# A kernel that plans its own order of issue: the planner's durations taken from a trace, and new ranks of its streams

## The chip, the cores and the metric

The kernel runs on one core of one Trainium2 chip. The metric is the device time of one execution in microseconds (us); the kernel before takes 4853.1 us, the median of three executions (4836.61 to 4856.57). Five engines work side by side on a core, each through its own instructions in the order in which they stand in the program: TensorE (PE, matrix products into the accumulator memory PSUM), VectorE (DVE), ScalarE (ACT), GpSimd (POOL), and SyncE (SP), which here only issues data transfers. An instruction that needs another engine's result waits on a semaphore, and everything behind it in its own engine's queue waits too.

## The reference

The batch is 32 images of 56 x 56 positions with 96 channels, float32. Two layers follow each other. Cut to what matters:

```python
# layer 0: a convolution block with weights mixed per image
pooled = jnp.mean(x, axis=(1, 2))
rw  = sigmoid(pooled @ Wr + br)                       # 4 mixing weights per image
h   = relu(bn(x @ mix(rw, Wpw)))                      # 96 -> 384 channels
h   = relu(bn(depthwise3x3(h, mix(rw, Wdw))))         # 9 taps per channel
x   = x + bn(h @ mix(rw, Wpwl))                       # 384 -> 96
# layer 1: a Fourier block, then a feed-forward net; tokens are the 3136 positions
t = x.reshape(32, 3136, 96)
h = relu(bn(layernorm(t) @ w1))                       # 96 -> 192
X = fft(h, axis=tokens)
xr, xi = relu(X.real*r - X.imag*i + rb), relu(X.imag*r + X.real*i + ib)
t = t + bn(ifft(xr + 1j*xi).real @ w2)                # 192 -> 96
t = t + qlinear(relu(qlinear(layernorm(t), W1)), W2)  # 8-bit products, 96 -> 384 -> 96
```

## The kernel before

Every image passes through a chain of stages. Each stage is written as a Python generator, a *stream*, which yields before each step the engine that the step runs on, the events it needs and the buffers it takes. A small planner, `Plan`, steps through all streams while the program is being built. It keeps a clock per engine, adds an estimated duration for each recorded instruction, and always goes on with the stream whose next step can start earliest; among steps that could start equally early the lower *rank* (called priority) goes first. The order in which the planner takes the steps is the order in which the instructions stand in the program. The planner's clock does not exist on the chip: only its order does.

```python
class Plan:
    HOP = 0.12
    def tick(self, engine, us):
        start = max(self.free[engine], self.now)
        self.now = self.free[engine] = start + us
    def run(self):
        while self.streams:
            for stream in self.streams:
                ...                                   # ready: own step, events, buffers
                key = (max(ready, self.free[stream.engine]), stream.priority, ready)
                if best is None or key < best[0]: best = key, ready, stream
            ...
            self.now = ready
            self._advance(stream)                     # records the step's instructions
```

The estimated durations of the kernel before (n is the number of elements per partition):

```python
if self.engine == DVE:   ...; us = 0.15 + n / 1000.0     # f16 tensor_scalar: n halved
elif self.engine == ACT: us = 0.24 + n / 1250.0
elif self.engine == POOL: us = 0.2 + n * {"tensor_copy": 1.2, "memset": 0.6}.get(name, 2.4) / 1000.0
else:                    us = 0.08                       # SP: issue of a transfer
def arrives(nbytes, *key): plan.done(*key, late=2.5 + nbytes / 150e3)
```

The streams, by the names of the PSUM tiles that their TensorE work fills (these names stand in the profile):

```python
mixing      # DVE: pooled (sum of an image), PE ps_rw, ACT sigmoid, DVE: wk, small, wk2 (mixed weights)
expansion   # PE ps_pw  -> ACT hp            (96 -> 384, two parts p of each image)
tensor      # PE ps_dw  -> ACT h2            (7 of 11 blocks of the depthwise taps: 3 waves of 144 products)
vector      # DVE h2 = hp * weight + h2      (the other taps: 8 per group of blocks, 1792, 1344 or 896 wide)
projection  # PE ps_pwl -> DVE x             (384 -> 96, added to the image)
forward     # PE ps_t_a -> DVE st_a, dm_a -> ACT rstd_a; PE ps_w1 -> DVE ha; PE ps_a -> ACT g -> SP gd
frequencies # SP g2 <- gd; PE ps_b -> ACT z, mir; POOL mir; DVE mir, z; ACT mir; DVE z   (8 halves per image)
spectrum    # PE ps_w2 (needs z) -> ACT zo -> PE ps_c -> DVE zo -> SP yd                 (4 per image)
inverse     # SP yt <- yd; PE ps_d -> DVE x; PE ps_t_f -> ACT, DVE, ACT yt; PE ps_n -> ACT n8
            # PE ps_f1 -> ACT h16 -> DVE h16 -> POOL h8; PE ps_f2 -> ACT y16 -> DVE y16 -> POOL x -> SP out
```

In the profile both `ps_w1` and `ps_w2` stand as `ps_w` (told apart by their inputs), `ps_f1` and `ps_f2` as `ps_f`, and the names lose their image numbers. Buffers are scarce on purpose: four PSUM buffers of two banks, two `mir`, one `zo`, four `h16`, two images' worth of `z`.

```python
plan = Plan(ps=4, mir=2, zo=1, h16=4)
...
Q.dma_start(yds[b][...], zo[:, 0:nk, :])
plan.release("zo", plan.now + 2.0)
...
("loads", 0, loads()), ("mixing", 0, mixing()), ("inverse", 1, inverse(0)),
("inverse", 1, inverse(1)), ("frequency loads", 0, frequency_loads()),
("frequencies", 2, frequencies()), ("forward", 3, forward(0)),
("forward", 3, forward(1)), ("projection", 4, projection()),
("vector", 5, convolved_vector()), ("tensor", 5, convolved_tensor()),
("expansion", 6, expansion()),
```

Of the kernel before, what the change touches and what calls it, by code (L numbers as in the profile page):

```python
# [46 lines left out]
NE = 4  # L47
C = 96
# [81 lines left out]
class Plan:  # L130
# [7 lines left out]
    HOP = 0.12  # L138

    def __init__(self, **buffers):  # L140
        self.free = dict.fromkeys((PE, DVE, ACT, POOL, SP), 0.0)
        self.now = 0.0
        self.events = {}
        self.streams = []

        self.buffers = {tag: [0.0] * n for tag, n in buffers.items()}
        self.busy = dict.fromkeys(self.free, 0.0)

    def tick(self, engine, us):
        start = max(self.free[engine], self.now)  # L150
        self.now = self.free[engine] = start + us
        self.busy[engine] += us
# [14 lines left out]
    def spawn(self, name, priority, gen):  # L167
        stream = Stream(name, priority, gen, self.now + self.HOP)
        self.streams.append(stream)
        self._advance(stream)  # L170

    def _advance(self, stream):
        now = self.now
        try:
            stream.wants(next(stream.gen))
        except StopIteration:
            self.streams.remove(stream)
        stream.ready = self.now + self.HOP
        return now

    def run(self):
        while self.streams:
            best = None
            for stream in self.streams:
                if any(len(self.buffers[tag]) < n for tag, n in stream.takes.items()):
                    continue
                ready = stream.ready
                missing = False
                for key in stream.after:
                    at = self.events.get(key)  # L190
                    if at is None:
                        missing = True
                        break
                    ready = max(ready, at + self.HOP)
                if missing:
                    continue
                for tag, n in stream.takes.items():
                    ready = max(ready, self.buffers[tag][n - 1])
                key = (max(ready, self.free[stream.engine]), stream.priority, ready)
                if best is None or key < best[0]:  # L200
                    best = key, ready, stream
            if best is None:
                raise RuntimeError(
                    "no stream can go on: "
                    + "; ".join(
                        f"{s.name} {[k for k in s.after if k not in self.events]} {s.takes}"
                        for s in self.streams
                    )
                )
            _, ready, stream = best  # L210
            for tag, n in stream.takes.items():
                del self.buffers[tag][:n]
            self.now = ready
            self._advance(stream)


def _size(ap):
    return int(np.prod(ap.shape[1:]))


class Engine:


    def __init__(self, plan, engine, namespace):
        self.plan, self.engine, self.namespace = plan, engine, namespace

    def __getattr__(self, name):
        def issue(out, *args, **kw):
            n = _size(out)
            if self.engine == DVE:  # L230
                if name in ("tensor_reduce", "bn_stats"):
                    n = _size(args[0])
                elif name == "reciprocal":
                    n *= 4
                elif name in ("tensor_scalar", "tensor_copy") and out.dtype == F16:
                    n *= 0.5
                us = 0.15 + n / 1000.0
            elif self.engine == ACT:
                us = 0.24 + n / 1250.0
            elif self.engine == POOL:  # L240
                us = 0.2 + n * {"tensor_copy": 1.2, "memset": 0.6}.get(name, 2.4) / 1000.0
            else:
                us = 0.08
            self.plan.tick(self.engine, us)
            return getattr(self.namespace, name)(out, *args, **kw)  # L245

        return issue


@with_exitstack  # L250
def kernel(
# [227 lines left out]
    def as_halves(ap):  # L479
# [3 lines left out]
    V, A, P, Q = (  # L483
        Engine(plan, DVE, nc.vector), Engine(plan, ACT, nc.scalar),
# [12 lines left out]
    def transpose(to, ap, eye):  # L497
        plan.tick(PE, 0.09)
        nc.tensor.transpose(to, ap, eye)

    def arrives(nbytes, *key):
        plan.done(*key, late=2.5 + nbytes / 150e3)
# [10 lines left out]
    def mixing():  # L513

        for b in range(NB):
# [4 lines left out]
            V.tensor_scalar(pool_b, ones, pooled, 1.0 / N, ALU.mult, ALU.mult)  # L520
# [14 lines left out]
            for e in range(1, NE):  # L535
                V.scalar_tensor_tensor(wk, wpw_s[:, e, :], rw[:C, e : e + 1], wk, ALU.mult, ALU.add)
# [3 lines left out]
            V.tensor_mul(prod, stk_s, by.to_broadcast([128, NMIX, NE + 1]))  # L540
            small = mixp.tile([128, NMIX], F32, tag="small", name=f"small_{b}")
            V.tensor_reduce(small, prod, AX.X, ALU.add)
# [8 lines left out]
            for e in range(1, NE):  # L551
                V.scalar_tensor_tensor(wk2, wpwl_s[:, e], rw[:, e : e + 1], wk2, ALU.mult, ALU.add)
# [30 lines left out]
    def expansion():  # L583

        for b, p, before in parts_of_all():
            xb = xpad[b % 3]
            for c in (2, 0, 1):

                for part, (at, ns) in enumerate(((0, (9, 9)), (18, (8, 8) if p == 0 else (8,)))):
# [10 lines left out]
                    plan.spawn("evac pw", 0, expanded(b, p, c, part, at, ns, ps))  # L600
# [17 lines left out]
    def convolved_tensor():  # L618

        for b, p, before in parts_of_all():  # L620
            for i, wave in enumerate(WAVES[p]):
# [5 lines left out]
                for t in range(9):  # L627
                    w, h = divmod(t, 3)
                    for q, (c, k) in enumerate(wave):
                        for g in range(G):  # L630
# [10 lines left out]
                                share=13.5,  # L641
# [4 lines left out]
                plan.spawn("evac dw", 0, convolved(b, p, i, wave, ps))  # L646
# [15 lines left out]
    def convolved_vector():  # L662

        for b, p, before in parts_of_all():
            for c, k0, nk in ON_VECTOR[p]:
# [6 lines left out]
                for t in range(9):  # L672
# [7 lines left out]
                    else:  # L680
                        V.scalar_tensor_tensor(to3, seen, weight, to3, ALU.mult, ALU.add)
# [39 lines left out]
    def moments(name, xt, s, who, out, kept=None):  # L721
# [21 lines left out]
        V.tensor_sub(d, st[:, :, 1], st[:, :, 4])  # L743
        V.tensor_add(v, st[:, :, 2], st[:, :, 5])
        V.scalar_tensor_tensor(d, d, C / 4.0, d, ALU.mult, ALU.mult)
        V.tensor_add(v, v, d)
# [65 lines left out]
    def frequencies():  # L812

        n = 0
        for b in range(NB):
            for i, (k0, nk) in enumerate(GROUPS):
# [9 lines left out]
                plan.spawn("spectrum", 1, spectrum(n, b, i, k0, nk))  # L826
                n += 1

    def nonlinearity(n, b, k0, nk, h, ps):
# [32 lines left out]
        V.scalar_tensor_tensor(zr, zr, 2.0, mr, ALU.mult, ALU.max)  # L862
        V.scalar_tensor_tensor(zi, zi, 0.0, mi, ALU.max, ALU.subtract)
# [3 lines left out]
    def imaginary_parts(n, h, im, zi, mi, col, used):  # L867
        yield DVE
        V.scalar_tensor_tensor(mi, im, col(nrd), zi, ALU.mult, ALU.add)
        V.scalar_tensor_tensor(zi, im, col("rd"), zi, ALU.mult, ALU.add)  # L870
# [3 lines left out]
    def spectrum(n, b, i, k0, nk):  # L874
# [37 lines left out]
        plan.release("zo", plan.now + 2.0)  # L912
        arrives(4 * PB * GK * C, "yd", b, i)

    def inverse(parity):


        for b in range(NB):
            for s in range(parity, NS, 2):
# [25 lines left out]
                V.tensor_add(nm, st[:, :, 1], st[:, :, 4])  # L945
                V.scalar_tensor_tensor(nm, nm, -0.5, rstd, ALU.mult, ALU.mult)
# [18 lines left out]
                for c in range(NC3):  # L965
# [8 lines left out]
                    plan.spawn("hidden", 0, hidden(parity, b, s, c, ps, h8))  # L974
# [38 lines left out]
    with tc.manual_schedule():  # L1013
        for name, priority, stream in (
            ("loads", 0, loads()), ("mixing", 0, mixing()), ("inverse", 1, inverse(0)),
            ("inverse", 1, inverse(1)), ("frequency loads", 0, frequency_loads()),
            ("frequencies", 2, frequencies()), ("forward", 3, forward(0)),
            ("forward", 3, forward(1)), ("projection", 4, projection()),
            ("vector", 5, convolved_vector()), ("tensor", 5, convolved_tensor()),
# [118 lines left out]
```

## Time and profile before

| | before |
|---|---|
| time, median of 3 | 4853.1 us |
| span of the profiled execution | 4857.6 us, 113896 instructions |
| TensorE (PE) busy | 4384.4 us, 90% |
| VectorE (DVE) busy | 3640.3 us, 75% |
| ScalarE (ACT) busy | 2774.1 us, 57% |
| GpSimd (POOL) busy | 1091.4 us, 22% |
| granted TensorE clock, mean | 0.944 of full speed |
| bytes moved | 339.06 MB, 70 GB/s |

All work of an image is recorded through two helper lines, so the line numbers of the profile say little; the tile names say which stage an instruction belongs to. TensorE's busy time is the union of its matrix products' recorded durations. A product takes longer in the record than it holds up its successor, because products are pipelined, so 90% busy does not say that 10% is all that can be won. Busy time of the other engines is closer to work done.

The waits are inferred: an engine's idle time is put down to whichever semaphore came last. "issue" is time in which an engine waited for nothing the profile shows.

### The profile page before, as it was taken

The numbers are of one execution on the slowest core, as the hardware profiler recorded it, in microseconds if no ns is written. First come the engines' busy times: TensorE is split into PE (matmuls) and PEld (weight loads), VectorE is DVE, ScalarE is ACT, GpSimd is POOL, SyncE is SP. The second block draws the span as 40 slices with busy tenths as digits, with TensorE's granted clock in tenths as the row PEclk, the third lists the DMA queues.
The fourth block names the chain that finished last, engine by engine and source line by source line (L and its number), as shares of the span: only waits on it lengthen the run. The fifth ranks groups of instructions, "written<-read, shape, count | busy, mean of one in ns | idle before, by whom it ended". The sixth has DMA issues, their size and how long they took to land.

```text
span 4857.6 us, 113896 instructions
## 1 busy us (share of the span) xinstructions
PE 4384.4 (90%) x47942; PEld 3137.0 (65%) x47942; DVE 3640.3 (75%) x7474; ACT 2774.1 (57%) x4391; POOL 1091.4 (22%) x1074
## 2 busy tenths in 40 slices
PE   5999989999898999989999899999989999999986
PEld 2666666666666666667666666666666666666664
DVE  5777778777877777867778787777877778687763
ACT  2556556665565655656555566655656556565544
POOL 1021212212122221322212122121222212222122
PEclk9999999999999999999999999999999999999986
DMA  3122223222222222222222232222222222222221
GB/s 83 56 76 70 58 69 84 67 68 70 60 79 73 67 71 72 60 80 75 76 63 65 69 85 66 68 70 60 79 73 68 70 75 62 80 73 73 63 70 43
DMA packets 304472, 339.06 MB, mean 70 GB/s; under 512 B 126836, under 2 KB 243476, under 8 KB 300660
## 3 DMA queue, kind: packets, MB, share of 16 engines
q1 hardware_dynamic: 303960, 331.77, 24.9%
q8 instruction: 377, 6.18, 0.5%
q14 instruction: 135, 1.11, 0.1%
HBM read 163.98 MB, written 158.27 MB: 66 GB/s over the span
## 4 chain that ended last, share of the span: by engine, by line
PE 64%; DVE 16%; ACT 12%; issue 5%; DMA 2%; POOL 0%; SPq 0%; ACTq 0%; POOLq 0%; DVEq 0%
PE ps_dw L495 14%; PE ps_pwl L495 10%; PE ps_pw L495 10%; PE ps_w L495 8%; DVE h L245 6%; PE ps_a L495 5%; PE ps_b L495 5%; PE ps_f L495 4%; DVE z L245 4%; ACT h L245 3%; PE ps_d L495 2%; ACT yt L245 2%; PE ps_c L495 2%; DVE wk L245 2%; DVE mir L245 1%
## 5 line engine op out<-in xcount | busy, mean ns | idle before, releaser
L245 DVE SCALAR_TENSOR_TENSOR h<-hp,small,h 128x1792 f32<-128x1792 f32 (+2 forms) x768 | 1269.7, 1653 | 28.4 <-ACT h L245 14.7
L495 PE MATMUL ps_dw<-hp,diag 32*32 32x448 f32 x27648 | 879.0, 545 | 42.9 <-issue 20.2
L245 POOL CAST h<-h 128x784 fp8e5<-128x784 f16 x384 | 489.7, 1295 | 1356.9 <-DVE h L245 1356.2
L495 PEld LDWEIGHTS ps_dw<-hp,diag 32*32 32x32 f32 x27648 | 536.0, 103 | 336.9 <-issue 121.9
L495 PE MATMUL ps_pw<-x,wk 96*128 96x504 f32 (+1 forms) x1344 | 657.9, 625 | 60.3 <-ACT g L245 35.3
L495 PE MATMUL ps_pwl<-h,wk 128*96 128x448 f32 x1344 | 532.3, 544 | 10.6 <-ACT h L245 10.6
L245 ACT ACTIVATE hp<-ps_pw,small 128x1008 f32<-128x1008 f32 (+2 forms) x384 | 363.3, 960 | 305.1 <-PE ps_pw L495 303.3
L495 PEld LDWEIGHTS ps_pw<-x,wk 96*128 96x128 f32 x1344 | 268.4, 210 | 307.9 <-issue 223.3
L495 PEld LDWEIGHTS ps_w<-w_s,z 96*112 96x112 f32 x3712 | 429.8, 196 | 45.2 <-DVE h L245 18.5
L495 PEld LDWEIGHTS ps_b<-dftb_s,g 112*96 112x96 f32 x3712 | 410.4, 173 | 66.8 <-ACT h L245 24.7
L495 PE MATMUL ps_b<-dftb_s,g 112*96 112x112 f32 x3712 | 430.1, 271 | 25.3 <-ACT h L245 13.7
L495 PE MATMUL ps_w<-w_s,z 96*112 96x96 f32 x3712 | 436.8, 281 | 7.6 <-DVE z L245 3.4
L245 ACT ACTIVATE h<-ps_dw,small 128x448 f32<-128x448 f32 x384 | 228.3, 635 | 356.4 <-PE ps_dw L495 356.1
L245 POOL TENSOR_TENSOR mir<-mir,z 96x392 f32<-96x392 f32 (+1 forms) x256 | 283.3, 1109 | 655.5 <-ACT mir L245 554.8
L245 DVE SCALAR_TENSOR_TENSOR ha<-ps_w,rstd_a,nshift 112x192 f32<-112x192 f32 x896 | 312.7, 407 | 109.1 <-PE ps_w L495 109.1
L495 PEld LDWEIGHTS ps_pwl<-h,wk 128*96 128x96 f32 x1344 | 215.5, 164 | 268.2 <-issue 243.3
L495 PE MATMUL ps_a<-ha,dfta_s 112*116 112x192 f32 x1792 | 369.1, 352 | 21.5 <-DVE ha L245 17.5
L245 ACT ACTIVATE z<-ps_b,vec_s 96x392 f32<-96x392 f32 (+1 forms) x512 | 335.1, 683 | 66.7 <-PE ps_b L495 66.2
L245 ACT ACTIVATE yt<-yt,nm,rstd_f 112x96 f32<-112x96 f32 x896 | 333.8, 456 | 54.8 <-DVE nm L245 52.8
L495 PE MATMUL ps_w<-w1c,x 96*112 96x192 f32 x1792 | 339.5, 333 | 18.6 <-ACT g L245 12.4
L495 PEld LDWEIGHTS ps_a<-ha,dfta_s 112*116 112x116 f32 x1792 | 315.2, 195 | 40.0 <-PE ps_rw L495 12.8
L245 ACT CAST h<-ps_f 128x784 f16<-128x784 f32 x384 | 302.5, 814 | 58.4 <-PE ps_f L495 50.0
(134 smaller groups left out, 6028.8 us busy)
## 6 DMA issues: line engine op xcount, KB each, us to landing
g<-gd SPq DMA_DIRECT2D x96, 588.0 KB
gd<-g SPq DMA_DIRECT2D x128, 336.0 KB
x<-in_x_dram SPq DMA_DIRECT2D x32, 1176.0 KB
yt<-yd SPq DMA_DIRECT2D x128, 294.0 KB
out_dram<-x SPq DMA_DIRECT2D x128, 294.0 KB
gd<-g SPq DMA_DIRECT2D x128, 252.0 KB
yd<-zo SPq DMA_DIRECT2D x96, 294.0 KB
g<-gd SPq DMA_DIRECT2D x32, 672.0 KB
```

The source lines that it names most:

```text
L245: return getattr(self.namespace, name)(out, *args, **kw)
L495: nc.tensor.matmul(to, lhsT, rhs, start=start, stop=stop)
```

## The change

No instruction is added or removed and no tile changes its size: on every engine the same instructions with the same operands stand in another order. Two things decide that order, and both change.

First, the planner's model of the chip. Durations are written anew per operation (for VectorE 0.13 us, or 0.08 us for small ones, plus n/960; the float16 `tensor_scalar` counts a quarter of its elements; for ScalarE different fixed parts for copies, and 1.28 us where the activation table has to be changed; an issue of a transfer by SyncE counts 0.36 us where it counted 0.08). The single `HOP` of 0.12 us after every step is replaced by a tail per engine, after which a result can be used, while the engine itself is free earlier; within VectorE a dependent instruction is made to wait for the tail (`behind`). [...] Transfers are taken to arrive sooner, and `zo` to come free later.

Second, the ranks: the mixing of the next image's weights falls from first to last, the emptying of the expansion's PSUM from 0 to 6, the loads of the frequency stage from 0 to 5, and the vector taps (4) now come ahead of projection, tensor taps and expansion.

The diff, cut to its core:

```diff
-    HOP = 0.12
+    TAIL = {PE: 0.2, DVE: 0.12, ACT: 0.14, POOL: 0.1, SP: 0.0}
...
-    def tick(self, engine, us):
-        start = max(self.free[engine], self.now)
-        self.now = self.free[engine] = start + us
+    def tick(self, engine, us, port=False):
+        start = max(self.free[engine], self.ready)
+        if port:
+            lo, hi = self.port[POOL if engine == DVE else DVE]
+            if lo <= start < hi:
+                start = hi
+            self.port[engine] = (start, start + us)
+        self.free[engine] = start + us
+        self.now = max(self.now, start + us + self.TAIL[engine])
...
             if self.engine == DVE:
+                us = 0.13 if n > 32 else 0.08
...
-                us = 0.15 + n / 1000.0
+                elif name == "tensor_scalar" and out.dtype == F16:
+                    n, port = n / 4, True
+                us += n / 960.0
             elif self.engine == ACT:
-                us = 0.24 + n / 1250.0
+                us = 0.05 if name == "copy" else 0.24 if {"scale", "bias"} <= kw.keys() else 0.15
+                us += n / 1200.0
...
+                asked = [f for f in args[1:] if f in (AF.Sqrt, AF.Sigmoid)]
+                if asked and asked != self.loaded:
+                    us += 1.28
...
-                us = 0.2 + n * {"tensor_copy": 1.2, "memset": 0.6}.get(name, 2.4) / 1000.0
+                us = 0.1 + n * {"tensor_copy": 1.04, "memset": 0.6}.get(name, 2.3) / 1000.0
             else:
-                us = 0.08
+                us = 0.36
...
-        plan.done(*key, late=2.5 + nbytes / 150e3)
+        plan.done(*key, late=1.4 + nbytes / 220e3)
...
-                    V.scalar_tensor_tensor(to3, seen, weight, to3, ALU.mult, ALU.add)
+                    W.scalar_tensor_tensor(to3, seen, weight, to3, ALU.mult, ALU.add)
...
-        plan.release("zo", plan.now + 2.0)
+        plan.release("zo", plan.now + 2.6)
...
-                    plan.spawn("evac pw", 0, expanded(b, p, c, part, at, ns, ps))
+                    plan.spawn("evac pw", 6, expanded(b, p, c, part, at, ns, ps))
-                plan.spawn("evac dw", 0, convolved(b, p, i, wave, ps))
+                plan.spawn("evac dw", 3, convolved(b, p, i, wave, ps))
-                plan.spawn("spectrum", 1, spectrum(n, b, i, k0, nk))
+                plan.spawn("spectrum", 2, spectrum(n, b, i, k0, nk))
-                    plan.spawn("hidden", 0, hidden(parity, b, s, c, ps, h8))
+                    plan.spawn("hidden", 3, hidden(parity, b, s, c, ps, h8))
...
-            ("loads", 0, loads()), ("mixing", 0, mixing()), ("inverse", 1, inverse(0)),
-            ("inverse", 1, inverse(1)), ("frequency loads", 0, frequency_loads()),
-            ("frequencies", 2, frequencies()), ("forward", 3, forward(0)),
-            ("forward", 3, forward(1)), ("projection", 4, projection()),
-            ("vector", 5, convolved_vector()), ("tensor", 5, convolved_tensor()),
+            ("loads", 0, loads()), ("mixing", 7, mixing()), ("inverse", 2, inverse(0)),
+            ("inverse", 2, inverse(1)), ("frequency loads", 5, frequency_loads()),
+            ("frequencies", 3, frequencies()), ("forward", 3, forward(0)),
+            ("forward", 3, forward(1)), ("projection", 5, projection()),
+            ("vector", 4, convolved_vector()), ("tensor", 5, convolved_tensor()),
```

## The prediction

> **What bounds the kernel now.** I read the page first, for busy shares, clock and costly groups; then the chain that ended last in order of time, for the period; then the busy times in stretches cut at the stages of two images; last the timeline of the transfer queue. The page:
>
> ```profile
> PE 4384.4 (90%) x47942; PEld 3137.0 (65%) x47942; DVE 3640.3 (75%) x7474; ACT 2774.1 (57%) x4391; POOL 1091.4 (22%) x1074
> ...
> L245 DVE SCALAR_TENSOR_TENSOR h<-hp,small,h 128x1792 f32<-128x1792 f32 (+2 forms) x768 | 1269.7, 1653 | 28.4 <-ACT h L245 14.7
> ...
> L245 POOL CAST h<-h 128x784 fp8e5<-128x784 f16 x384 | 489.7, 1295 | 1356.9 <-DVE h L245 1356.2
> ```
>
> No engine is full, and the vector taps are a third of VectorE's work. In the chain of waits, these are first tensor waves (ps_dw) of images 4, 14, 16 and 30:
>
> ```profile
> 572.58 8.72 PE ps_dw L495 x282
> 2046.91 8.72 PE ps_dw L495 x281
> 2344.76 8.72 PE ps_dw L495 x281
> 4405.69 8.72 PE ps_dw L495 x281
> ```
>
> (4405.69 - 572.58) / 26 = 147.4 us per image. TensorE's own need is smaller. I take what a product adds when the stream is unbroken from pieces of the same chain (a wave of 144 products 8.72 us, six of ps_pwl 4.51, eight of ps_b 1.53, eight of ps_a 2.61, and so on) and times the products of one image: 125.4 us. So 22 us of each image are waits. To see where, I cut images 15 and 16 at the starts of their stages (columns: us, then busy PE, PEld, DVE, ACT, POOL, granted clock, DMA share, GB/s):
>
> ```profile
> 2231.20:2246.20 15.00, 14.97 (x68) 9.23 (x69) 9.03 (x34) 7.88 (x14) 4.63 (x6) 1.00 0.59 167
> 2269.00:2296.80 27.80, 25.40 (x414) 20.39 (x412) 25.86 (x43) 16.30 (x27) 12.59 (x10) 0.94 0.30 77
> 2304.90:2324.00 19.10, 14.38 (x60) 8.90 (x59) 18.71 (x25) 5.76 (x7) 2.35 (x3) 0.82 0.38 103
> ...
> 2375.30:2400.20 24.90, 24.79 (x112) 14.53 (x111) 12.13 (x51) 17.67 (x33) 4.63 (x7) 1.00 0.37 109
> 2400.20:2427.90 27.70, 23.24 (x388) 17.76 (x387) 25.47 (x48) 15.48 (x24) 12.24 (x8) 0.94 0.45 120
> ```
>
> Two kinds. In the first and fourth line TensorE is full and VectorE idles 6 and 13 us. In the other three, which lie in the frequency stage (ps_b, ps_w2, ps_c), VectorE is busy for 93%, 98% and 92% while TensorE waits and its clock falls. The kernel is bound alternately by TensorE and VectorE; what the order can win is to lay VectorE's work beside TensorE-heavy stretches. The third stretch holds the next image's mixed weights (pooled, wk), which had rank 0. The transfer queue adds a second loss:
>
> ```profile
> 2162.53 3.71 SPq L245 DMA_DIRECT2D wk<-wk  x6
> 2166.34 6.66 SPq L245 DMA_DIRECT2D yd<-zo  x2
> ```
>
> VectorE had finished zo at 2163.27 in its timeline; yd could be issued only at 2166.34, behind six copies of mixed weights, and ScalarE got the one zo buffer back at 2169.44: 3.1 us of queue, 3.1 us of flight. The old planner counts 0.08 us per issue and 2.0 us for the flight.
>
> [...] GpSimd's cast averages 1295 ns, and 0.84 us where nothing competes. [...] the granted clock is 0.82 in the stretch with the longest TensorE waits and 1.00 in full ones[...]. [...] the trace has 62 loads of 1283 ns, and their number does not change. [...] The trace has 0.42 us for 784 float16 elements where nothing competes, nearer the new planner's 0.33 + 0.12 than the old 0.54.
>
> **The change part by part.** No work goes; the sums per image stay. *Durations.* TensorE's entries were already right (8.12 us to 8.63 planned per wave, plus 0.4, against 8.72), so the model improves on the other engines: a cast on GpSimd 1.14 to 0.92 us (trace 0.84 free), an add of 784 elements 2.08 to 1.90 (1.68), a float16 operation as above, an issue 0.08 to 0.36 (trace 0.33). None makes an instruction faster; they make the planned overlap come true.
>
> *The new order.* I counted, in the built program, what stands on each engine between the same TensorE landmarks, and multiplied by busy time over count from the costly groups of the trace (tap of 1792: 549.9 / 256 = 2.15 us, of 1344 1.66, of 896 1.15; z update 0.65; ha 0.35; and so on). The rule tried is that a stretch lasts as long as its busiest engine. For the kernel before it can be tested: images 15 and 16 give 145.4 + 143.1 = 288.5 us, against the 290.35 us that these windows measure; stretch by stretch, for image 15, 16.7, 16.1, 15.0, 19.0, 4.6, 29.3, 6.5, 19.4, 18.8 against 17.65, 16.5, 15.0, 18.7, 4.1, 27.8, 8.1, 19.1, 20.6. Good enough to use. The kernel before alternates two patterns of order; the changed one repeats a single one:
>
> ```
> from            PE    DVE   ACT   longest
> first wave     15.1  16.0  10.5   16.0
> second wave    14.0   8.0   6.4   14.0
> ps_pwl (1st)   21.3  13.7  18.3   21.3
> ps_b (1st)     14.3  13.0  16.6   16.6
> ps_w2 (1st)     5.9   6.1   1.4    6.1
> ps_b (3rd)     17.8  18.9  10.8   18.9
> ps_w2 (3rd)     7.7   9.3   5.1    9.3
> ps_w2 (4th)    11.2  17.3   9.5   17.3
> ps_d           18.0  16.2  13.9   18.0   sum 137.5
> ```
>
> Before, the stretches that VectorE led held up to 34.7 us of its work beside 20.4 of TensorE; now the worst excess is 6 us. The sum falls from 144.3 (mean of 145.4 and 143.1) to 137.5. The rule was 147.4 - 144.3 = 3.1 us short of the true period; I add them and expect 140.6, that is 6.8 us less per image. Over the 28 images in steady state that is 190 us; filling and draining (the first three images, and the 300 us after image 31's first wave) I give 20 us for issue counted rightly and the mixed weights no longer ahead of waiting work. 4853 - 210 = 4643, rounded to 4645.
>
> *Ranks.* Mixing at 7 puts pooled beside the third wave, and wk behind the last z update. The six wk copies now stand after the four yt loads, so no yd waits for them. The taps at rank 4, in 500 runs instead of 381 of their 768, are spread more finely among other VectorE work.
>
> **The rivals.** *A new wait at the end of the frequency stage.* In the new order only 3.6 us of TensorE work lie between the last ps_b and the ps_w2 that needs it; before it was never under 9.8 us. The trace's durations make that link about 5.1 us (ScalarE 1.7, VectorE 1.24, ScalarE 0.86, VectorE 1.29), so TensorE should wait 1.5 us or more; then yd, yt and ps_d need about 7.5 us (zo copy 0.85, flight 3.1, issues 1.0, a second flight estimated at 2.5) with 6.4 us of TensorE work beside them. If both waits add to the table and halve the clock each time, the period is 145 and the time 4770. For it: VectorE is the longest there anyway. Against: partly it is the same idle time, counted once as VectorE's load. *The order hardly matters*, because the semaphores and four PSUM buffers force the same cycle: 4830. Against: the test above shows the time following the load. *The lock is worth more than I count*: VectorE's and GpSimd's operations no longer block each other, VectorE's sum shrinks, and the period comes within 8 us of TensorE's 125.4: 4460. For it: 0.45 us on each of 384 casts; against: casts stand off TensorE's path, and VectorE's taps average 2.15 us against 2.08 free, so little is there to win.
>
> **Range and chances.** The sum of longest engines is blind to what happens inside a stretch; its error on single stretches was up to 4 us, on an image about 3. An error of 4 us in the new period is 110 us. Better agreement of plan and chip pulls down, the thin links pull up, so 4530 to 4760. Faster by over 2% means under 4756, which needs 3.5 us of the 6.8: 0.79. Within 2%: 0.15. Slower needs the first rival twice over: 0.06.
>
> **What would show it.** Right: first waves about 140.6 us apart, all alike; PE busy within 100 us of 4384 or below, DVE busy near 3640, clock at or above 0.95; ScalarE's wait for yd (93.6 us now) halved; VectorE at most 95% busy in the frequency stage. The second rival shows as a period near 147, the first as TensorE idle before ps_w2 for z and before ps_d for yt, with the clock under 0.94 there. Wrong altogether: DVE busy up by over 100 us[...], or TensorE waiting for wk before ps_pw, because mixing now comes last.

## The result and the profile after

The changed kernel takes 4616.08 us, the median of four executions (4612.0 to 4619.96), against 4854.84 us for the kernel before on the same chip (4836.61 to 4870.68). The ratio is 0.951, with a 95% interval of 0.947 to 0.954.

From the page of the changed kernel, the busy time of each engine and the costliest rows of VectorE, TensorE and GpSimd:

```profile
PE 4293.7 (93%) x47942; PEld 3106.1 (67%) x47942; DVE 3601.7 (78%) x7474; ACT 2771.1 (60%) x4391; POOL 1039.5 (23%) x1074
...
L271 DVE SCALAR_TENSOR_TENSOR h<-hp,small,h 128x1792 f32<-128x1792 f32 (+2 forms) x768 | 1250.2, 1628 | 25.4 <-ACT h L271 15.7
L520 PE MATMUL ps_dw<-hp,diag 32*32 32x448 f32 x27648 | 849.1, 543 | 0.7 <-ACT mir L271 0.5
...
L271 POOL CAST h<-h 128x784 fp8e5<-128x784 f16 x384 | 389.6, 1034 | 806.3 <-DVE h L271 804.7
```

TensorE's records overlap: 27648 of ps_dw at 543 ns each are 15013 us, and their busy time is 849.1. The taps' do not: 768 at 1628 ns are 1250.3 us, with a busy time of 1250.2.

No work is gone: the counts of matmuls, vector and scalar instructions are those of before, and ScalarE's table loads (`ACT_TABLE_LOAD`) are 62 of 1283 ns in both traces. VectorE was busy for 38.6 us less, 1.2 us an image; the time fell by 239. So the instructions hardly became shorter. They wait less. The chain that ended last, in order of time, shows where a period begins (start, us, engine, tile, line, count); here are the first waves of images 14, 15 and 16:

```profile
1948.16 8.72 PE ps_dw L520 x281
...
2088.16 8.72 PE ps_dw L520 x281
...
2228.04 8.72 PE ps_dw L520 x281
```

The distance is 140.0 us. I laid TensorE's order beside its trace and read off the start of each image's first wave: over the 28 images from 3 to 31 the period is 139.7 us on average (138.0 to 140.3), where the kernel before had 147.6 (142.8 to 153.0). The 28 periods save 222 us. The start, up to image 3's first wave, fell from 419.5 to 413.3 us, and what follows the start of image 31's from 305.7 to 293.3: another 18.6. Together that is the difference of the two spans, 4857.6 and 4617.0.

Image 16, cut at the nine stages of the prediction's table (us, then busy PE, PEld, DVE, ACT, POOL, granted clock, DMA share, GB/s):

```profile
2228.00:2243.80 15.80, 15.54 (x336) 11.07 (x338) 15.73 (x16) 9.98 (x19) 7.89 (x4) 1.00 0.09 26
2243.80:2257.80 14.00, 14.00 (x331) 10.64 (x331) 8.65 (x14) 5.72 (x8) 4.27 (x4) 1.00 0.18 52
...
2280.30:2295.90 15.60, 14.81 (x95) 11.05 (x96) 12.14 (x20) 13.32 (x21) 8.85 (x9) 1.00 0.50 140
2295.90:2301.90 6.00, 6.00 (x50) 5.38 (x49) 5.96 (x9) 3.60 (x4) 0.05 (x1) 1.00 0.83 197
2301.90:2320.00 18.10, 18.10 (x371) 14.53 (x370) 17.49 (x29) 9.03 (x16) 2.07 (x3) 1.00 0.15 38
2320.00:2328.50 8.50, 7.84 (x64) 7.36 (x63) 8.03 (x14) 5.47 (x9) 2.03 (x2) 1.00 0.16 38
2328.50:2347.30 18.80, 16.56 (x57) 11.46 (x55) 14.67 (x23) 8.76 (x10) 2.43 (x4) 0.73 0.36 98
2347.30:2368.00 20.70, 18.69 (x119) 11.95 (x135) 16.30 (x60) 13.84 (x23) 0.15 (x1) 1.00 0.06 15
```

In every stretch but one TensorE is busy for 90% or more, at full clock, and in four of the nine VectorE is busy for 94% or more as well. One stretch still looks like the old kernel: the fourth ps_w2 (18.80 us), with TensorE at 88%, VectorE at 78% and the clock at 0.73. TensorE's waits of the whole run name what ends it (us in total, times, longest):

```profile
PE ps_w L520 <- DVE z L271: 72.3, 59, 3.5
PE ps_t_f L524 <- ACT h L271: 54.3, 28, 2.3
...
PE ps_d L520 <- DMA yt<-yd: 32.8, 29, 7.3
```

The page parts the first of them by input: 53.5 us belong to ps_w2, the rest to ps_w1, which doesn't read z:

```profile
L520 PE MATMUL ps_w<-w_s,z 96*112 96x96 f32 x3712 | 455.4, 287 | 53.8 <-DVE z L271 53.5
```

Of the 32.8 us of ps_d, 14.9 fall into the last three waits, where the program drains; the 26 before them are 0.7 us each. Before, ps_w waited 3.4 us for z and ps_d 15.1 for yt (all of it in three waits at the end). In place of them stood:

```profile
PE ps_f L495 <- DVE z L245: 81.6, 29, 3.3
PE ps_c L495 <- ACT zo L245: 56.4, 42, 4.2
```

The transfer queue of the changed kernel:

```profile
2201.10 0.32 SPq L271 DMA_DIRECT2D yd<-zo  x1
2203.98 1.40 SPq L271 DMA_DIRECT2D yt<-yd  x4
2206.54 3.71 SPq L271 DMA_DIRECT2D wk<-wk  x6
```

The six weight copies stand behind the yt loads, and yt is issued 2.88 us after yd. ScalarE's wait for yd to leave the zo buffer is down from 93.6 to 28.4 us.

### The profile page after: what moved, and what is told of

It reads as the page before. It is cut to its first block, busy times and chain, and to the rows that moved or that the text cites. A ratio compares the mean times of both kernels' runs of the same rounds, so it can differ in the third digit from the quotient of the medians.

```text
span 4617.0 us, 114190 instructions
## 1 busy us (share of the span) xinstructions
PE 4293.7 (93%) x47942; PEld 3106.1 (67%) x47942; DVE 3601.7 (78%) x7474; ACT 2771.1 (60%) x4391; POOL 1039.5 (23%) x1074
## 4 chain that ended last, share of the span: by engine, by line
PE 75%; DVE 13%; ACT 8%; issue 2%; DMA 1%; SPq 0%; POOL 0%; POOLq 0%; ACTq 0%; DVEq 0%
PE ps_dw L520 17%; PE ps_w L520 14%; PE ps_pwl L520 11%; PE ps_pw L520 7%; DVE h L271 7%; PE ps_a L520 6%; PE ps_b L520 6%; PE ps_c L520 4%; PE ps_f L520 3%; PE ps_d L520 2%; ACT h L271 2%; ACT mir L271 2%; PE ps_n L524 2%; ACT z L271 2%; PE ps_t_f L524 2%
## 5 line engine op out<-in xcount | busy, mean ns | idle before, releaser
L271 DVE SCALAR_TENSOR_TENSOR h<-hp,small,h 128x1792 f32<-128x1792 f32 (+2 forms) x768 | 1250.2, 1628 | 25.4 <-ACT h L271 15.7
L520 PE MATMUL ps_dw<-hp,diag 32*32 32x448 f32 x27648 | 849.1, 543 | 0.7 <-ACT mir L271 0.5
L520 PE MATMUL ps_pw<-x,wk 96*128 96x504 f32 (+1 forms) x1344 | 580.2, 575 | 6.6 <-DVE wk L271 5.4
L271 POOL CAST h<-h 128x784 fp8e5<-128x784 f16 x384 | 389.6, 1034 | 806.3 <-DVE h L271 804.7
L520 PE MATMUL ps_pwl<-h,wk 128*96 128x448 f32 x1344 | 555.4, 563 | 6.3 <-ACT h L271 4.4
L520 PE MATMUL ps_w<-w_s,z 96*112 96x96 f32 x3712 | 455.4, 287 | 53.8 <-DVE z L271 53.5
L520 PE MATMUL ps_b<-dftb_s,g 112*96 112x112 f32 x3712 | 395.8, 262 | 29.9 <-ACT y L271 21.1
L520 PEld LDWEIGHTS ps_b<-dftb_s,g 112*96 112x96 f32 x3712 | 377.7, 164 | 65.8 <-ACT y L271 30.0
L271 POOL TENSOR_TENSOR x<-x,y 96x784 f32<-96x784 f32 x128 | 275.2, 2150 | 435.9 <-DVE y L271 419.2
L271 ACT ACTIVATE h<-h,small 128x1792 f32<-128x1792 f32 (+2 forms) x96 | 135.9, 1416 | 374.1 <-DVE h L271 374.1
L520 PE MATMUL ps_w<-w1c,x 96*112 96x192 f32 x1792 | 335.4, 330 | 23.1 <-DVE z L271 18.8
```

What stands on the lines that cost most here:

```text
L520: nc.tensor.matmul(to, lhsT, rhs, start=start, stop=stop)
```

## The experiments

Two theories on what carries the gain. *Load*: a stretch lasts as long as its busiest engine, so any order with a small sum of busiest engines is fast, however it came about. *Honest durations*: the gain is in the model; only with it do the planned order and the chip's order fit. To judge the first I count, as in the prediction, the sum of busiest engines per image for every order (an estimate from counts in the built program and durations in traces; one and the same order came out at 138.4 and 137.5 with different cuts). Here are all runs; the period is read as above, as a mean over 28 images (smallest to largest):

```
                                      us      ratio (95%)            sum    period
before                              4855       1                     144.3  147.6 (143 to 153)
changed                             4616.1   0.951 (0.947 to 0.954)  137.5  139.7 (138 to 140)
before + new ranks                  4936.3   1.016 (1.013 to 1.018)  138.4  150.5 (148 to 157)
changed + old ranks                 4969.6   1.023 (1.020 to 1.025)  148.1  151.5 (132 to 167)
changed, mixing at rank 0           4827.3   0.993 (0.991 to 0.996)  147.2  147.2 (143 to 155)
before, mixing at rank 7            4911.3   1.010 (1.007 to 1.014)  140.8  149.8 (132 to 166)
before + new ranks, copies later    4771.8   0.980 (0.978 to 0.982)  137.5  144.7 (142 to 156)
changed, transfers as before        4820.5   0.993 (0.990 to 0.996)  144.0  146.5 (136 to 158)
changed, port not planned           4929.7   1.014 (1.010 to 1.017)  144.0  151.2 (111 to 175)
changed, fewer taps, frequency      4522.9   0.931 (0.929 to 0.934)  134.1  136.3 (135 to 137)
changed, fewer taps, second wave    4618.1   0.951 (0.949 to 0.953)  137.5  139.7 (138 to 140)
searched ranks                      4658.6   0.957 (0.955 to 0.959)  136.6  141.4 (138 to 146)
searched ranks, copies later        4627.9   0.952 (0.950 to 0.954)  136.6  140.0 (137 to 144)
searched ranks, yt first            4588.9   0.943 (0.941 to 0.946)  136.6  138.7 (136 to 143)
```

Each ratio is against the kernel before on the same chip in the same comparison (4855 to 4869 us there).

### The two halves, each alone

The new ranks in the kernel before:

```diff
-            ("loads", 0, loads()), ("mixing", 0, mixing()), ("inverse", 1, inverse(0)),
+            ("loads", 0, loads()), ("mixing", 7, mixing()), ("inverse", 2, inverse(0)),
 ...                                     (all ranks of the change, durations as before)
```

> The kernel before with the new ranks alone[...]. Theory A, load: the time follows the sum, over the stretches between the same TensorE landmarks, of the busiest engine's work. That sum is 138.4 us per image for this order (before 144.2, after 137.6), so the period should be about 141 us and the time 4640, nearly the whole gain. Theory B, honest durations: the gain comes from a plan that agrees with the chip, so with the old durations the time stays near before, 4780 to 4900.

Measured: 4936.3 us. Load is wrong here by 300 us, although its sum is nearly that of the changed kernel. Honest durations was right that the gain is missing, but the time lies 36 us above its range too. The longest wait of TensorE and the transfer queue of this kernel show one reason:

```profile
PE ps_d L495 <- DMA yt<-yd: 170.7, 32, 7.4
```

```profile
2349.90 0.33 SPq L245 DMA_DIRECT2D yd<-zo  x1
2355.34 3.71 SPq L245 DMA_DIRECT2D wk<-wk  x6
2359.15 1.62 SPq L245 DMA_DIRECT2D yt<-yd  x4
```

The six copies stand ahead of yt in a queue that keeps its order. They first wait for the weights (VectorE finishes wk at 2355.31 us in its timeline) and then take 0.62 us each, where the plan counted 0.08. So yt is issued 9.25 us after yd, not 2.88.

The new durations with the old ranks (the same lines, the other way round, in the changed kernel):

> The changed kernel's durations, latencies and port, with the ranks of the kernel before. Theory A: the sum of the busiest engines is 148.1 us per image (three patterns of order in turn), above before's 144.2, so the time is 4900 to 4990, slower than before. Theory B: most of the gain is here, 4640 to 4700.

Measured: 4969.6 us, period between 132 and 167. Load is right, and honest durations, taken as a gain of its own, is refuted: the better model with the old ranks is 2.3% slower than the kernel before. Neither half is worth anything alone. Alone they cost 1.6 and 2.3%; together they bring 4.9%.

### One rank

Mixing put back to rank 0 in the changed kernel, and mixing alone put to rank 7 in the kernel before:

```diff
-            ("loads", 0, loads()), ("mixing", 7, mixing()), ("inverse", 2, inverse(0)),
+            ("loads", 0, loads()), ("mixing", 0, mixing()), ("inverse", 2, inverse(0)),
```

> The changed kernel with one rank put back: mixing of the next image's weights at 0 in place of 7. Theory A: the sum of the busiest engines is 147.2 us per image, so the time is near 4900. Theory B: one rank of a tie-break changes little while the durations are right, 4610 to 4680.

Measured: 4827.3 us. In the changed kernel one rank is worth 211 us, most of the gain. Load has the direction and missed by 70 us, since here the period (147.2) doesn't exceed the sum; the other theory, that a rank changes little, is out.

> The kernel before with one rank changed: mixing at 7 in place of 0. Theory A: the sum of the busiest engines is 140.8 us per image on average (irregular, from 131 to 149), so the time is about 4730. Theory B: without the new durations nothing is won, 4830 to 4880.

Measured: 4911.3 us. The same rank in the old model costs 1%. Load missed by 180 us here too, and honest durations by 31. The longest wait is ps_c for zo (59.5 us), but the kernel before has 56.4 there, so it doesn't account for the loss; its cause stays open.

### The transfer queue alone

In the kernel before with the new ranks, the copies are held back in the plan until the yt loads of the image ahead are issued. Every other engine keeps exactly its order, over the whole program (the sum in the table moves by 0.9 only because the program is cut at other places):

```diff
-            yield SP
+            yield SP, [("yt read", b - 2, s) for s in range(2) if b >= 2]
             wk2s[b] = [wk2]
```

> The kernel before with the new ranks (e1, 4936 us), and the six copies of a mixed weight now held back in the plan until the yt loads of the image ahead are issued; the order on TensorE is that of e1, only the transfer queue is rearranged. Queue theory (e1 lost its gain because six copies of 0.62 us each stood ahead of yt, where the plan counted 0.08 each): the wait of ps_d for yt, 170.7 us in e1, falls to 30 or less, and the time to 4740 to 4800. Rival (the order on the engines themselves is at fault, made by a model that doesn't know the durations; the wait for yt only gathers what would be lost elsewhere): the wait falls, others grow, and the time stays within 1% of e1, 4890 to 4960.

Measured: 4771.8 us. TensorE's waits:

```profile
PE ps_w L495 <- DVE z L245: 97.9, 56, 3.5
...
PE ps_n L499 <- ACT yt L245: 44.2, 29, 4.0
...
PE ps_d L495 <- DMA yt<-yd: 18.8, 5, 7.2
```

The wait of ps_d falls by 152 us and the time by 165. That is shown: no other engine's order moved. (The time falls by more than the wait, although 33.4 us of ps_t_f appear; the mean granted clock rises from 0.937 to 0.947 with it.) About half of what the new ranks lacked in the old model was the place of six copies in one queue. The other half, 156 us up to the changed kernel at the same sum of 137.5, isn't at one place: ps_w2 waits 44 us more for z (97.9 against 53.5), ps_n 36 more for yt, and the rest is spread. What it comes from stays open.

### Parts of the model

The transfers planned as before, in the changed kernel:

```diff
-                us = 0.36
+                us = 0.08
-        plan.done(*key, late=1.4 + nbytes / 220e3)
+        plan.done(*key, late=2.5 + nbytes / 150e3)
-        plan.release("zo", plan.now + 2.6)
+        plan.release("zo", plan.now + 2.0)
```

> The changed kernel with the transfers alone planned as before (0.08 us of issue, 2.5 us and bytes over 150e3 of flight, zo free 2.0 us after its issue)[...]. Load theory (a stretch lasts as long as its busiest engine; the sum is 144.0 us an image in this order against 137.5 in the changed kernel, 144.3 before): 4800 to 4860, as before. Queue theory (the half of the gain that e1 missed is in the transfers alone, because their waits end the frequency stage): also a loss, with the wait of ps_d for yt at 100 us or more. Rival (durations of the engines carry the gain, the transfers are small): 4620 to 4700, and waits on transfers under 60 us.

Measured: 4820.5 us, with ps_d waiting 36.9 us for yt. Load is right; the wait of 100 us or more on the queue isn't there. The transfer entries matter by the order that they bring about, whose sum is 144.0 again and which varies from image to image.

The entry `port` not planned. In the changed kernel the planner doesn't let an instruction of VectorE with two operands in on-chip memory (object `W`), or a float16 `tensor_scalar`, start within one of GpSimd other than a memset, nor the other way round. Here it does:

```diff
-        if port:
+        if False:
```

> [...] Load theory (sum of busiest engines 144.0 us an image, irregular from image to image): 4790 to 4860. Port theory (what matters is that the casts are kept out of VectorE's long instructions): the mean cast on GpSimd goes back from 1034 to 1250 ns or more, the mean tap instruction stays at 1628 ns within 2%, and the time is above 4700 for that reason. Rival (the port entry is worth little): cast below 1100 ns and 4610 to 4680.

Measured: 4929.7 us; the cast takes 1165 ns, the tap 1650. All three expectations miss: the cast lies between the two limits, and the time above the ranges of load and rival. (The port theory's time above 4700 came true, but without the cast of 1250 ns or more that was to be its reason.) The order became irregular (periods from 111 to 175 us), so this run doesn't measure the entry by itself. The searched ranks below do better: there the cast takes 1263 ns, almost as long as before (1295), in a kernel faster than the changed one. A short cast isn't what carries the gain.

### The load itself

Two runs keep every other engine's order, and leave out instructions of VectorE while the plan still counts them. Both leave out part of the convolution, so they are no candidates; their time alone is of interest.

```diff
+                        W.mute = p == 1 and c == 1 and t in (3, 4, 5, 6)   # or: p == 0 and t in (7, 8)
                         W.scalar_tensor_tensor(to3, seen, weight, to3, ALU.mult, ALU.add)
+                        W.mute = False                                     # muted: planned, not issued
```

> The changed kernel, with every instruction in its place, except that VectorE leaves out four tap instructions of 128x896 (1149 ns each, 4.6 us an image) near the end of the frequency stage, three of them in the stretch from the first ps_w2 of the fourth group to the first ps_d, where VectorE is the busiest engine (17.3 us against 11.2 of TensorE; the stretch took 18.4 us). Load theory (a stretch lasts as long as its busiest engine): 3.4 us an image less, about 97 us, so 4500 to 4540. Rival 1 (the chain through z, its evacuations and the transfers sets the end of that stretch, not VectorE's load): 4590 to 4620. Rival 2 (what counts is VectorE's work as a whole, backlog carried over): 4480 to 4540 here, and as much in the run with taps left out in the second wave.

> The changed kernel, with every instruction in its place, except that VectorE leaves out two tap instructions of 128x1792 (2126 ns each, 4.25 us an image, nearly as much as in the other run) in the second wave of the depthwise convolution, where TensorE is the busiest engine (14.0 us against 8.0 of VectorE). Load theory: nothing changes, 4600 to 4625. Rival 2 (VectorE's work as a whole): 4480 to 4540.

Measured: 4522.9 and 4618.1 us. The period falls from 139.7 to 136.3 in the first, by the 3.4 us that the sum gives up, and by nothing in the second, although 4.25 us of VectorE's work are gone. Both are as load said: of these two places, VectorE's work counts in the one where VectorE leads, and not in the other. Where the 3.4 us come off is not quite where the table had them. The end of the taps in the changed kernel, by the timeline (start, us, engine, operation, tile, count, idle before and what ended it):

```profile
2346.28 4.71 DVE L271 SCALAR_TENSOR_TENSOR h<-hp,small,h 128x896 f32<-128x896 f32 x4
...
2347.27 2.90 PE L520 MATMUL ps_d<-dftd_s,yt 116*96 116x112 f32 x28 [0.47 <-DMA yt<-yd]
2350.91 1.97 DVE L271 SCALAR_TENSOR_TENSOR x<-ps_d,cb,x 96x784 f32<-96x784 f32 x2
2351.03 1.04 ACT L271 ACTIVATE h<-h,small 128x896 f32<-128x896 f32 x1 [3.18 <-DVE h L271]
2352.08 0.35 PE L524 MATMUL ps_t_f<-ident,x 96*112 96x96 f32 x2 [1.92 <-ACT h L271]
```

and the same place with four taps less:

```profile
2301.74 2.90 PE L523 MATMUL ps_d<-dftd_s,yt 116*96 116x112 f32 x28 [0.88 <-DMA yt<-yd]
...
2303.33 1.03 DVE L274 SCALAR_TENSOR_TENSOR x<-ps_d,cb,x 96x784 f32<-96x784 f32 x1 [2.47 <-PE ps_d L523]
2304.50 0.51 PE L527 MATMUL ps_t_f<-ident,x 96*112 96x96 f32 x4
```

In the changed kernel VectorE still works off four taps when ps_d begins. The sum of ps_d and x (96x784), which ps_t_f reads, stands behind them in VectorE's order, and ps_t_f starts 4.81 us after ps_d. ScalarE's relu of the taps ends at the same time, which is presumably why the profile puts the wait down to h: ps_t_f doesn't read h. With the taps gone, VectorE waits for ps_d, and ps_t_f comes 2.76 us after it. The stretch of ps_d gives back about 2.2 us, the one before it 1.2. So ps_t_f's wait for h, 54.3 us in the run, is load that spilled over the border of a stretch.

### A better set of ranks

I searched ranks for the earliest end by the plan's own clock, which is no device time. The core of what it found:

```diff
-            ("loads", 0, loads()), ("mixing", 7, mixing()), ("inverse", 2, inverse(0)),
+            ("loads", 2, loads()), ("mixing", 8, mixing()), ("inverse", 0, inverse(0)),
-            ("inverse", 2, inverse(1)), ("frequency loads", 5, frequency_loads()),
+            ("inverse", 0, inverse(1)), ("frequency loads", 3, frequency_loads()),
-            ("frequencies", 3, frequencies()), ("forward", 3, forward(0)),
+            ("frequencies", 1, frequencies()), ("forward", 4, forward(0)),
-            ("vector", 4, convolved_vector()), ("tensor", 5, convolved_tensor()),
+            ("vector", 8, convolved_vector()), ("tensor", 4, convolved_tensor()),
 ...         (evac pw 2, evac dw 8, evac prj 4, diagonals 6, spectrum 1, imaginary parts 3, expansion 7)
```

> The changed kernel's model with another set of ranks, chosen for the earliest end by the plan's own clock (4418 us there against 4479 for the changed kernel's ranks). Load theory: sum of busiest engines 136.6 us an image against 137.5, so 4570 to 4620. If the plan's clock is right to its difference: 4540 to 4570. Rival (the plan's clock is trusted beyond what it knows, above all for the six weight copies, which stand ahead of the last yd in this order and take 0.62 us each where the plan has 0.36): waits of ps_d for yt above 80 us, and 4640 to 4720.

Measured: 4658.6 us, as the rival said, with ps_d waiting 85.0 us for yt. The six copies were again ahead of the last yd. I took them for the cause once more, so the next run issues them later, and leaves every other engine's order as it is:

```diff
-                    Q.dma_start(wk2q[to], wk2[at, 0:NPE])
+                    plan.tick(SP, 0.36)
+                    later.append((b, wk2q[to], wk2[at, 0:NPE]))     # issued behind yt of image b - 2, s = 1
```

> The searched ranks (4658.6 us) with the same order on all engines, and only the six weight copies issued later, behind the yt loads instead of ahead of them and of the last yd. Queue theory: the wait of ps_d for yt falls from 85 us to 20 or less, and 60 to 85 us come off: 4575 to 4605, faster than the changed kernel's 4616. Load theory without a queue (sum 136.6 us an image against 137.5): 4570 to 4600, the same. Rival (the wait only moves to the next link, ps_c for zo or ps_w for z): 4630 to 4660.

Measured: 4627.9 us, with ps_d still waiting 72.3 us. The gain is 31 us where 60 to 85 were expected, and the time is a little below the rival's range: the copies were not the main obstacle. In the run with the copies ahead they had ended at 2228.42 us, VectorE's copy into zo at 2228.60, and yd went at 2228.63, hardly late; there too two stores stood between yd and yt. The queue of the new run:

```profile
2208.30 0.30 SPq L271 DMA_DIRECT2D yd<-zo  x1
2212.67 0.69 SPq L271 DMA_DIRECT2D gd<-g  x2
2213.53 1.43 SPq L271 DMA_DIRECT2D yt<-yd  x4
2215.29 3.71 SPq L543 DMA_DIRECT2D wk<-wk  x6
```

The obstacle is the pair of stores of g. They wait for ScalarE, whose copy of g ran from 2211.85 to 2212.65, and yt stands behind them: it is issued 5.23 us after yd. The last run issues these stores behind yt too:

```diff
-                    Q.dma_start(gd[0:PB, at : at + nq, :], g[0:PB, 0:nq, :])
-                    Q.dma_start(gd[PB:PA, at : at + nq, :], g[PB:PA, 0:nq, :])
+                    late = s == 1 and q0 == 0 and b > 0 and (b - 1, 1) not in seen_yt
+                    ...                     # late: planned here, issued behind yt of image b - 1, s = 1
```

> The searched ranks again with the same order on every engine, and the transfer queue alone rearranged once more: in the run before (4627.9 us) two gd stores stood between the last yd and the yt loads and waited for g; yt was issued 5.2 us after yd's issue where the changed kernel has 2.9. Here yt goes first, then gd, then the six weight copies. Queue theory: yt is issued some 2.3 us earlier an image, the wait of ps_d for it falls from 72 us to 15 or less, and about 60 us come off: 4560 to 4590, below the changed kernel's 4616. Rival (the wait moves on to ps_c for zo, ps_w for z or ps_f for h, as most of it did when the weight copies were moved): 4605 to 4635.

Measured: 4588.9 us, ratio 0.943 (0.941 to 0.946), below the changed kernel's interval of 0.947 to 0.954 (the two didn't run side by side). The wait of ps_d for yt is 15.7 us, about its expected size, and 15.3 of it fall into the draining at the end. The gain is 39 us, not 60, and a part of the wait moved on to the next link, which had 1.7 us in the run before:

```profile
PE ps_t_f L524 <- DVE x L271: 37.0, 31, 1.5
```

## Why the prediction was right

**The period.** Its sum of busiest engines, 137.5, and the shortfall of 3.1 gave 140.6 us; measured were 139.7. The shortfall is 3.3 in the kernel before and 2.2 after. Times 28 images, 6.8 us were expected to save 190 and 7.9 saved 222. This makes up the 29 us by which the time came out below 4645. (The 3.5 us that the prediction named for a gain of 2% leave its own 20 us of filling and draining out; with them 2.8 would do.)

**Filling and draining.** Allowed 20 us, measured 18.6.

**Stretch by stretch.** For image 16 the table had 16.0, 14.0, 21.3, 16.6, 6.1, 18.9, 9.3, 17.3, 18.0 and the trace has 15.8, 14.0, 22.5, 15.6, 6.0, 18.1, 8.5, 18.8, 20.7. Six stretches are within 1 us. The last two, 4.2 us too short, hold what the table can't see: the wait for z, and the taps that run over into ps_d. In all, the table is 5.4 us too short in three stretches and 2.9 too long in five; that the constant of 3.1 us taken over from the kernel before covers the difference is in part luck.

**The clock.** The sum has no term for it. The granted clock averaged 0.944 over 4857.6 us before and 0.957 over 4617.0 after, which is 272 and 199 us of full speed withheld. So some 70 of the 240 us may have come through the clock (an estimate from these means, at most so much, as TensorE isn't always what is waited for). No run parts this share from the load; in the prediction it is hidden in the 3.1 us.

**The rival of new waits** was real, at about the size worked out by the prediction: for z it wanted 1.5 us or more, and the fourth ps_w2 of image 16 waits 1.77 (53.5 us in the whole run, 3.4 before); for yt it had 7.5 us against 6.4 of cover, and ps_d waits 0.7 an image in the steady state, not 1.1. (Of the 7.5 us, 2.5 were its own guess at the second flight. In the trace after, yt's four issues end at 2345.29 us and ps_d begins at 2347.27, 1.98 us behind them.) The clock falls to 0.73 in that stretch, below the 0.94 it named. What failed of it is only the sum: it wanted a period of 145, and the waits are there, with a clock of 0.50 for 10.24 us behind the first in image 16, while the period is 2.2 us above the sum. So they don't come on top of VectorE's load in full, which was the prediction's argument against this rival. The second rival, that the order hardly matters (4830, a period near 147), is out.

**The signs.** Waves alike: yes. PE busy within 100 us of 4384 or below: 4293.7. DVE busy near 3640: 3601.7. Clock at or above 0.95: 0.957. ScalarE's wait for yd halved: 28.4 of 93.6. VectorE at most 95% busy in the frequency stage: true of the stage as a whole, 87% (12.14, 5.96, 17.49, 8.03 and 14.67 us in 67.0), but not of two of its stretches, 97% (17.49 of 18.10) and 99% (5.96 of 6.00). That sign was set too strictly: TensorE is full there as well (18.10 and 6.00 us, where the table had 17.8 and 5.9 of its own need). Of the signs of being wrong altogether neither came: ps_pw waits for wk 5.4 us in two waits.

**The lock.** The trace of the kernel before shows what the prediction meant by it on casts and taps. Of the casts, 31 ran beside no VectorE instruction and took 0.84 us on average; 46 began within a tap, took 2.16 to 3.17 us, and ended 0.70 us or more after that tap. One of each (start, us):

```profile
2390.92 0.84 POOL L245 CAST h<-h 128x784 fp8e5<-128x784 f16 x1 [0.84 <-DVE h L245]
...
2402.99 1.61 DVE L245 SCALAR_TENSOR_TENSOR h<-hp,small,h 128x1344 f32<-128x1344 f32 x1
2403.14 2.50 POOL L245 CAST h<-h 128x784 fp8e5<-128x784 f16 x1 [4.00 <-DVE h L245]
```

Taps of 1792 took 2.33 us beside GpSimd's work (75 of them) and 2.07 without it (181). What makes the one wait for the other isn't shown. The third rival, that these waits are worth more than counted, is out: the cast fell by 261 ns on each of 384, the tap by 25, VectorE's busy time by 1.2 us an image.

**What was right for a reason that holds less far than I thought.** The prediction took the sum of busiest engines as the rule, and the durations as what makes the planned overlap come true. The runs bear out the rule as a lower bound, within the 1 us or so of the sum itself: no order's mean period fell below its sum (one equals it), and of the taps left out only those counted where VectorE leads. But an order can lie far above it: the new ranks in the old model have a sum of 138.4 and a period of 150.5. For the changed kernel the rule was good because its links are nearly covered. I hadn't shown that before, except for two of them.

Durations alone did not make the planned overlap come true: with the old ranks they cost 2.3%. What stays open is how much each of them brings. Every part put back (transfers, port, one rank) lost 200 us or more, far more than the parts can add up to, since each made the planner fall into another cycle of order. The ranks fit this model; the runs don't tell what any entry is worth apart from that.

## What to carry to other kernels

With a planner that picks greedily, a more honest model is no gain by itself, and neither are new ranks: judge model and ranks as a pair, by the order that they produce. Cut that order at the stages of one image and add up the busiest engine of each; in the kernels before and after it gives the period to 2.2 and 3.3 us here, and far less than the truth where a link is exposed (12 us less in one order). Then look at every in-order queue for what stands ahead of a load on the critical link: moving six copies was worth 165 us in one kernel, six copies and two stores 70 in another, with no other engine's order touched.

## What the runs showed of the hardware that I hadn't expected

Issues in the transfer queue differ by kind: yd, yt and gd take 0.32 to 0.33 us each in it (medians in the traces before and after), and the copies of weights from one on-chip tile to another 0.59 (3.71 for six in the lines above). And the clock behind one and the same short wait differs. After 1.77 us of waiting for z, the fourth ps_w2 of image 16 took 5.17 us for its last 26 records (the profile shows two for each of these products, 3712 for the program's 1856) in the changed kernel, and 4.36 with the taps left out. Both kernels in that place, cut by time (columns as above):

```profile
2330.60:2335.60 5.00, 4.98 (x27) 4.98 (x27) 4.48 (x9) 2.88 (x4) 0.00 (x0) 0.50 0.15 54
```

```profile
2286.20:2290.40 4.20, 4.16 (x27) 4.16 (x27) 3.71 (x8) 2.90 (x4) 0.00 (x0) 0.62 0.18 65
```

TensorE is busy throughout, at a mean granted clock of 0.50 and 0.62. The record of the clock has just two values in the traces before and after, 0.50 and 1.00 (56 stretches of each in the changed kernel). It goes to 0.50 at 2330.49 us for 10.24 us in the first kernel, and at 2287.18 for 6.83 us in the second, so a wait of 1.77 us was followed by about four to six times as long at half clock. The two waits of TensorE just before were of 0.66 and 1.77 us. How long a wait has to be for the clock to fall, and what sets the length of the slow stretch, the runs don't show.
